# Two seams of a three-stage attention kernel: gate placement, early pools, split softmax, mixing rows stored in SBUF

## The chip, the cores and the metric

The kernel runs on one core of a Trainium2 chip. A core has a matrix engine (TensorE, PE in the profile; its weight loads are shown as PEld), a vector engine (VectorE, DVE), an activation engine (ScalarE, ACT), a general engine (GpSimd, POOL) and a queue engine that issues most of the DMA transfers (SyncE, SP). They run side by side and wait for one another through semaphores; each takes its instructions strictly in the order in which they were put in its queue. SBUF is the on-chip memory of 128 partitions, PSUM the banks into which PE writes. The metric is the device time of one launch in microseconds (us); the time before is the median of three runs.

## What is computed

Input `x` is 4 x 192 x 128 x 128 in float32 (images, channels, rows, columns). Two layers follow each other. Cut to what matters:

```python
# layer 0: attention between channels (8 heads of 24 channels), over all 16384 pixels
q, k, v, l = split(depthwise3x3(conv1x1(x, w_qkv)), 4)
q = q / max(norm(q over pixels), 1e-12);  k likewise
attn = softmax((q @ k.T) * temperature)              # 24 x 24 for each image and head
t = fc2(relu(fc1(mean of l over the pixels)))
L = t * sigmoid(t)                                   # the gate, one number for each image and channel
y = conv1x1(L + attn @ v + x, w_proj) + L
# layer 1: neighbourhood attention, 6 heads, 3x3 neighbours at dilation 1, 2, 3, reflected borders
h = y + depthwise3x3(y, pos_w) + pos_b
q, k, v = conv1x1(h, qkv_w)
out = conv1x1(neighbourhood attention of q, k, v, proj_w)
```

## The kernel before

There are three stages, and each has to end, or nearly, before the next can begin.

**Stage 1, `project` (L220) and `plan_projection` (L260).** The images are taken in two pairs, and a pair in 32 bands of four rows: 64 bands n = 0 to 63. `loads` brings a band of x (`xt`, L272 and L274, three transfers; four buffers); PE makes q, k, v of it (`pu`, L280 to L294); ACT copies q and k (`us`, five buffers) and SP stores them to `qk_dram`; v goes into a ring of rows (`vboth`, `ring2`), and its depthwise 3x3 is run there, for most channels by DVE as one operation for each tap (`tap`, L327: accumulator `pa` and, at the last tap, `v_False`; the band's centre tap is ACT's, L320) and for the rest by ACT and POOL (`v_True`). The results go to `v_dram`. The order of instructions inside the stage is planned by hand: class `Schedule` (L35) takes items with engines, costs and due times and lists them, and class `Stage` (L137) owns the stage's pools and emits the list. Outside of such a plan the framework's own scheduler orders the instructions, and it may put a transfer whose memory is free among the transfers of an earlier stage.

Ahead of the stage the main function and `project` load all weights that they need, with those of the gate and `wp1`, `wp2` among them (L199, L207): eighteen transfers issued before the first `xt`. The rings are set to zero whole by POOL (L251). During the stage the sums of x that the gate needs are collected (`xsum`, `xcol`, `xrow`). After the plan has been emitted comes the gate, `gate_bias` (L448), once for each pair of images: sums over the taps; `pl`, four matmuls for each image (L471, L472), multiplied by DVE (L473); mean; `pf`, `pf2`, the two small layers (L479, L484); sigmoid by ACT (L487); `pb` (L494), which brings the gate through the projection, and a copy to `bias` (L495). Each step waits for the one before. It uses PSUM of its own, two banks.

**Stage 2, `channel_attention` (L498).** For each of eight heads `convolved` (L527) is run for q and for k. It makes the depthwise 3x3 as banded matmuls: six steps c2, each with a tile of band matrices (`band`, L538) and a tile of rows (`u`, L541), both in pools of three buffers; for each two channels 24 matmuls into two PSUM tiles `pc` (L554, pool of four banks), which ACT copies (L563) and of which DVE takes the statistics (L565, for the norms). These ACT copies come in groups of four. `cut_rows` (L577) handles the two rows where the halves of the image meet. `products` (L618) multiplies q and k over all pixels (`gram`, L623, 128 matmuls), adds up the parts (`kept`, `part`, `extra`, `own`), and brings sums and squared norms through one PSUM tile `sm` (L645) into `logits`, `nk`, `nq` (L654 to L656).

When all eight heads are done, the softmax of all of them runs at once (L665 to L682: square root, maximum, reciprocal, three multiplications, maximum, subtraction, exponential, sum, reciprocal, multiplication). Then for each image the attention matrices go through the projection (`pm`, L689, two heads a PSUM tile), DVE copies them to `mixed` (L690, one buffer), and three transfers bring them to `mix_dram` and from there to `mix1` (rows 0 to 127) and `mix2` (64 rows behind `wp2`), L691 to L693. `mix1` and `mix2` hold the matrix by which one product takes the place of attention times v and projection.

**Stage 3, `second_pass` (L696).** Its own pools, its own plan. It loads the second layer's weights (L716 to L718), adds 1 to the centre tap (L719), sets its rings and `parts` to zero whole (L729, L1012), and then again walks over 64 bands: x and v of the band (`xv`, eight buffers, L733 to L744), the product with `mix1`, `mix2`, `wp1` (`ph`, L754), evicted by ACT with the gate's `bias` added (L758, `hboth`), positional taps, q, k, v, scores, softmax, sums over neighbours, output. The pools of this stage, and those of stage 2, take the memory that the stage before has used.

Of the kernel before, what the change touches and what calls it, by code (L numbers as in the profile page):

```python
# [14 lines left out]
HEADS0 = 8  # L15
# [19 lines left out]
class Schedule:  # L35
# [6 lines left out]
    def __init__(self):  # L42
        self.ops, self.pools = [], {}
# [93 lines left out]
class Stage:  # L137


    def __init__(self, ctx, tc, prefix, sbuf, psum):  # L140
        self.nc, self.bufs = tc.nc, {**sbuf, **psum}
        self.schedule, self.tiles, self.written, self.readers = Schedule(), {}, {}, {}
        self.pools = {}
        for n, k in self.bufs.items():
            space = dict(space=bass.MemoryType.PSUM) if n in psum else {}
            self.pools[n] = ctx.enter_context(tc.tile_pool(name=prefix + n, bufs=k, **space))
# [39 lines left out]
HALVES = [slice(0, G), slice(G, 128)]  # L186
AROUND = (0, 1, 2, 6, 7, 8, 3, 5)
# [3 lines left out]
def channel_attention_then_dilated_attention(ctx: ExitStack, tc: tile.TileContext, d, out: bass.AP):  # L191
# [10 lines left out]
    wp1 = load(const, "wp1")  # L202
    mix1, mix2, biases = [], [], []
    for b in range(B):
        mix1.append(const.tile([128, C], F32, tag=f"mix1{b}", name=f"mix1{b}"))
        mix2.append(const.tile([128, C], F32, tag=f"mix2{b}", name=f"mix2{b}"))
        nc.sync.dma_start(mix2[b][0:G], d["wp2"])  # L207
# [5 lines left out]
    mix_dram = dram.tile([B, C, C], F32, tag="mix_dram", name="mix_dram")  # L213

    project(tc, d, x, load, qk_dram, v_dram, v2_dram, biases)
    channel_attention(tc, d, load, qk_dram, mix_dram, mix1, mix2)
    second_pass(tc, d, x, load, wp1, mix1, mix2, biases, v_dram, v2_dram, out)


def project(tc, d, x, load, qk_dram, v_dram, v2_dram, biases):  # L220

    nc = tc.nc
    with ExitStack() as ctx:
        wts = ctx.enter_context(tc.tile_pool(name="p1w", bufs=1))
        st = ctx.enter_context(tc.tile_pool(name="p1s", bufs=2))

        wx, wx2, wv2, dwv = (load(wts, n) for n in ("wx", "wx2", "wv2", "dwv"))
        wl, wl2, dwl = load(wts, "wl"), load(wts, "wl2"), load(wts, "dwl")  # L230
        wprojI, wprojT = load(wts, "eye"), load(wts, "wprojT")
        fc1T, bfc1, fc2T, bfc2 = (load(wts, n) for n in ("fc1T", "bfc1", "fc2T", "bfc2"))
        nc.vector.tensor_add(wprojI, wprojI, wprojT)
        sums = []
        for p in range(B // 2):
            xsum = st.tile([128, 3, NB], F32, tag="xsum", name=f"xsum{p}")
            xcol = st.tile([128, 3, 2, H], F32, tag="xcol", name=f"xcol{p}")
            xrow = st.tile([128, 3, 3], F32, tag="xrow", name=f"xrow{p}")
            nc.gpsimd.memset(xrow, 0.0)
            sums.append((xsum, xcol, xrow))  # L240

        with ExitStack() as inner:
            stage = Stage(
                inner, tc, "p1", dict(xt=4, us=5, v=3, v2=3, side=3, ring=1), dict(pu=6, pa=1)
            )
            rings = stage.pools["ring"]
            vboth = rings.tile([128, RING + SPARE, 2, W + 2], F32, tag="vboth", name="vboth")
            ring = [vboth[:, :, 0], vboth[:, :, 1]]
            ring.append(rings.tile([128, RING + SPARE, W + 2], F32, tag="ring2", name="ring2"))
            for r in (vboth, ring[2]):  # L250
                nc.gpsimd.memset(r, 0.0)  # L251
            plan_projection(nc, stage, x, wx, wx2, wv2, dwv, vboth, ring, sums, qk_dram, v_dram, v2_dram)
            stage.run(tc)

        ps_g = ctx.enter_context(tc.tile_pool(name="p1pg", bufs=2, space=bass.MemoryType.PSUM))
        for p in range(B // 2):
            gate_bias(nc, st, ps_g, p, *sums[p], wl, wl2, dwl, fc1T, bfc1, fc2T, bfc2, wprojI, biases[p])
# [189 lines left out]

def gate_bias(nc, st, ps_g, p, xsum, xcol, xrow, wl, wl2, dwl, fc1T, bfc1, fc2T, bfc2, wprojI, bias):  # L448


    small = lambda shape, name: st.tile(shape, F32, tag=name, name=f"{name}{p}")
    tot = small([128, 3], "tot")
# [13 lines left out]
    for im in range(2):  # L466
        half = slice(im * G, (im + 1) * G)
        pl = ps_g.tile([HALF, 2, NT], F32, tag="pg", name=f"pl{p}_{im}")
# [8 lines left out]
    pf = ps_g.tile([RED, 2], F32, tag="pg", name=f"pf{p}")  # L477
# [4 lines left out]
    pf2 = ps_g.tile([HALF, 2, 2], F32, tag="pg", name=f"pf2{p}")  # L482
# [6 lines left out]
    pb = ps_g.tile([128, NG], F32, tag="pg", name=f"pb{p}")  # L489
# [8 lines left out]
def channel_attention(tc, d, load, qk_dram, mix_dram, mix1, mix2):  # L498
# [7 lines left out]
    with ExitStack() as ctx:  # L506
        wts = ctx.enter_context(tc.tile_pool(name="paw", bufs=1))
        band_p = ctx.enter_context(tc.tile_pool(name="pab", bufs=3))
        u_p = ctx.enter_context(tc.tile_pool(name="pau", bufs=3))
        cut_p = ctx.enter_context(tc.tile_pool(name="pac", bufs=1))  # L510
        q_p = ctx.enter_context(tc.tile_pool(name="paq", bufs=1))
        k_p = ctx.enter_context(tc.tile_pool(name="pak", bufs=1))
        st = ctx.enter_context(tc.tile_pool(name="pas", bufs=1))
# [5 lines left out]
        same, fold, ones, ident = load(wts, "same"), load(wts, "fold"), load(wts, "ones"), load(wts, "ident")  # L519
        wph, tempr = load(wts, "wph"), load(wts, "temp")  # L520
# [97 lines left out]
        def products(hd, q, sq, k, sk, cut):  # L618
# [25 lines left out]
            sm = ps_s.tile([CH0, 2 * B * CH0 + B], F32, tag="sm", name=f"sm{hd}")  # L644
# [12 lines left out]

        for hd in range(HEADS0):
            q, sq = convolved(hd, 0, q_p)
            k, sk = convolved(hd, 1, k_p)  # L660
            products(hd, q, sq, k, sk, cut_rows(hd, (sq, sk)))

        for n in (nq, nk):  # L665
            flat = n.rearrange("p b h -> p (b h)") if n is nq else n.rearrange("p b h c -> p (b h c)")
            nc.scalar.activation(flat, flat, AF.Sqrt)
            nc.vector.tensor_scalar_max(flat, flat, 1e-12)
            nc.vector.reciprocal(flat, flat)
        nc.vector.tensor_mul(nq, nq, tempr.unsqueeze(1).to_broadcast([CH0, B, HEADS0]))  # L670
        nh = B * HEADS0
        rows = logits.rearrange("p b h c -> p (b h) c")
        wide = lambda a: a.unsqueeze(2).to_broadcast([CH0, nh, CH0])
        nc.vector.tensor_mul(rows, rows, nk.rearrange("p b h c -> p (b h) c"))
        nc.vector.tensor_mul(rows, rows, wide(nq.rearrange("p b h -> p (b h)")))
        top, tot = fin.tile([CH0, nh], F32, tag="top", name="top"), fin.tile([CH0, nh], F32, tag="tot", name="tot")
        nc.vector.tensor_reduce(top, rows, AX.X, ALU.max)
        nc.vector.tensor_sub(rows, rows, wide(top))
        nc.scalar.activation(rows, rows, AF.Exp)
        nc.vector.reduce_sum(tot, rows, axis=AX.X)  # L680
        nc.vector.reciprocal(tot, tot)
        nc.vector.tensor_mul(rows, rows, wide(tot))  # L682
        for b in range(B):
            mixed = fin.tile([CH0, HEADS0, C], F32, tag="mixed", name=f"mixed{b}")
            for hd in range(0, HEADS0, 2):
                pm = ps_c.tile([128, B, W], F32, tag="pc", name=f"pm{b}_{hd}")
                two = pm.rearrange("p b w -> p (b w)")[:CH0, : 2 * C].rearrange("p (h o) -> p h o", h=2)
                for e in range(2):
                    nc.tensor.matmul(two[:, e, :], logits[:, b, hd + e, :], wph[:, hd + e, :], start=True, stop=True)  # L689
                nc.vector.tensor_copy(mixed[:, hd : hd + 2, :], two)  # L690
            nc.sync.dma_start(mix_dram[b].rearrange("(h c) o -> c h o", c=CH0), mixed)  # L691
            nc.sync.dma_start(mix1[b], mix_dram[b, 0:128, :])
            nc.sync.dma_start(mix2[b][G:128], mix_dram[b, 128:C, :])  # L693


def second_pass(tc, d, x, load, wp1, mix1, mix2, biases, v_dram, v2_dram, out):  # L696
# [4 lines left out]
    with ExitStack() as ctx:  # L701
# [6 lines left out]
                xv=8, y=3, y2=3, prod=3, middle=2, side=1, moved=1, term=4, acc=4, o=3, s_sb=1, e=2, mx=2, sm=2, e_sb=2,  # L708
            ),
            dict(pc=2, ex=2, q=1, pa=1, sc=1),  # L710
        )
        add, hold, tile_of, tiles = stage.schedule.add, stage.hold, stage.tile, stage.tiles
        fill, read, repeat, written = stage.fill, stage.read, stage.repeat, stage.written
        wts, rings = pool("p2w", 1), pool("p2r", 1)

        wq1, wq2, wkv, wkv2 = (load(wts, n) for n in ("wq1", "wq2", "wkv", "wkv2"))  # L716
        wo, wo2, posw, posb = (load(wts, n) for n in ("wo", "wo2", "posw", "posb"))
        pick, order, spread = (load(wts, n) for n in ("pick", "order", "spread"))  # L718
# [9 lines left out]
        for r in (hboth, hring[2]):  # L728
            nc.gpsimd.memset(r, 0.0)  # L729
# [281 lines left out]
        for t in parts:  # L1011
            nc.gpsimd.memset(t, 0.0)  # L1012
# [295 lines left out]
def build(arrays):  # L1308
    import concourse.bacc as bacc

    nc = bacc.Bacc("TRN2", target_bir_lowering=False, num_devices=1)
# [17 lines left out]
```

## Time and profile before

| | |
|---|---|
| median of three runs | 4686.12 us (4683.99 to 4691.63) |
| the profiled execution | 4694.5 us, its span 4692.7 us |
| mean granted TensorE clock | 0.979 |
| PE busy | 4494.9 us, 96% of the span |
| DVE, POOL, ACT busy | 3919.5 (84%), 3229.8 (69%), 2784.3 us (59%) |
| stage 1 | to about 857 us |
| stage 2 | 901 to about 1717 us, eight heads |
| stage 3 | from about 1765 us to the end |

The span is the time from the first to the last event of the profiled execution; the execution's own time is some 2 us longer. The page divides the span into 40 slices of 117.3 us and shows the busy share of each in tenths, where 9 is 90% or more. These are the rows of TensorE, the clock that it was granted, and what the transfers moved:

```profile
PE   8999999799999988999999999999999999999986
PEclk9999999899999988999999999999999999999997
DMA  7777777688877845444344444434444444443311
GB/s 225 244 242 234 237 238 237 165 186 183 181 170 163 179 100 136 91 105 101 91 95 104 101 98 100 105 93 97 105 96 97 105 101 91 107 102 89 91 43 30
```

The eighth slice (821 to 938 us) holds the first seam, the fifteenth (1642 to 1760 us) most of the second: there PE drops to 7 and 8 tenths. In slices of this width the rest is full. A TensorE that counts as busy isn't necessarily at its peak, since the records of matmuls overlap.

### The profile page before, as it was taken

What the parts mean: (1) busy time and instruction counts of PE and PEld (TensorE: products, weight loads), DVE (VectorE), ACT (ScalarE), POOL (GpSimd) and SP (SyncE); (2) the same over time, 40 slices, a digit from 0 to 9 for tenths busy, and PEclk for the clock granted to TensorE, in tenths of its full rate; (3) what the DMA queues carried; (4) which work ended last, traced back from release to release, by engine and by line L of the source; (5) the groups of instructions that cost most, each with busy time, mean ns of one, the idle gap of its engine ahead of it and who ended that gap; (6) DMA issues with size and microseconds to landing.
All of it is one profiled execution on the core that took longest, in us unless ns stands there. A gap on an engine that the chain in (4) does not pass through costs nothing.

```text
span 4692.7 us, 63172 instructions
## 1 busy us (share of the span) xinstructions
PE 4494.9 (96%) x20592; PEld 1640.0 (35%) x20592; DVE 3919.5 (84%) x5480; ACT 2784.3 (59%) x4759; POOL 3229.8 (69%) x2765
## 2 busy tenths in 40 slices
PE   8999999799999988999999999999999999999986
PEld 3333333344455442233333333333333333333321
DVE  6998899655444545899999999999999999999996
ACT  6888888666656646455455555555555555555531
POOL 6787778400000002788889999898899999999997
PEclk9999999899999988999999999999999999999997
DMA  7777777688877845444344444434444444443311
GB/s 225 244 242 234 237 238 237 165 186 183 181 170 163 179 100 136 91 105 101 91 95 104 101 98 100 105 93 97 105 96 97 105 101 91 107 102 89 91 43 30
DMA packets 496615, 628.31 MB, mean 134 GB/s; under 512 B 136144, under 2 KB 331036, under 8 KB 496288
## 3 DMA queue, kind: packets, MB, share of 16 engines
q1 hardware_dynamic: 476832, 524.40, 42.1%
q0 software_dynamic: 19456, 99.89, 11.1%
q8 instruction: 165, 2.70, 0.3%
q14 instruction: 162, 1.33, 0.1%
HBM read 297.18 MB, written 201.92 MB: 106 GB/s over the span
## 4 chain that ended last, share of the span: by engine, by line
PE 69%; DVE 14%; DMA 5%; issue 5%; POOL 3%; ACT 2%; SPq 1%; POOLq 0%; DVEq 0%; ACTq 0%
PE ph L754 9%; PE pc L554 8%; PE pu L280 7%; PE ex L1097 7%; PE sc L973 6%; DVE prod L962 6%; DVE term L1103 5%; PE pu L285 4%; PE gram L623 4%; PE po L1119 3%; PE po L1115 3%; PE pkv L896 3%; POOL acc L1106 3%; PE pu L413 2%; PE q L951 2%
## 5 line engine op out<-in xcount | busy, mean ns | idle before, releaser
L1106 POOL TENSOR_TENSOR acc<-acc,term 128x512 f32<-128x512 f32 x1536 | 1977.2, 1289 | 215.0 <-DVE term L1103 139.1
L1103 DVE TENSOR_TENSOR term<-ex,vring 128x512 f32<-128x512 f32 (+2 forms) x1596 | 1007.4, 661 | 67.0 <-PE ex L1097 39.7
L962 DVE TENSOR_TENSOR prod<-q,kring 128x1536 f32<-128x1536 f32 (+1 forms) x600 | 1008.3, 1686 | 34.0 <-ACT kring L914 13.9
L350 POOL TENSOR_TENSOR v_True<-v_True,side 128x512 f32<-128x512 f32 (+1 forms) x512 | 647.9, 1267 | 189.3 <-ACT side L339 162.2
L563 ACT COPY conv<-pc 128x512 f32<-128x512 f32 x384 | 511.2, 1501 | 267.1 <-PE pc L554 244.2
L327 DVE SCALAR_TENSOR_TENSOR pa<-vboth,dwv,pa 128x1024 f32<-128x1024 f32 (+1 forms) x448 | 574.3, 1282 | 86.2 <-ACT pa L320 56.0
L1097 PE MATMUL ex<-e_sb,spread 108*128 108x512 bf16 x1728 | 596.0, 387 | 46.2 <-DVE term L1103 20.7
L554 PE MATMUL pc<-u,band 64*64 64x508 f32 (+1 forms) x4608 | 581.5, 596 | 30.4 <-DMA band<-in_bands 12.1
L729 POOL MEMSET hboth<- 128x3900 f32 x1 | 3.3, 3347 | 874.9 <-DMA mix_dram<-mixed 874.9
L565 DVE BATCH_NORM_STATS2 stats<-pc 128x6 f32<-128x128 f32 x1536 | 341.9, 285 | 256.3 <-ACT conv L563 256.3
L809 DVE SCALAR_TENSOR_TENSOR pa<-hboth,posw,pa 128x1024 f32<-128x1024 f32 (+1 forms) x384 | 489.5, 1275 | 65.8 <-ACT pa L797 52.7
L973 PE MATMUL sc<-prod,pick 128*32 128x512 f32 x3456 | 483.8, 607 | 4.0 <-DVE e L1030 2.8
L1097 PEld LDWEIGHTS <-spread 108*128 108x128 bf16 x1728 | 149.1, 98 | 723.3 <-issue 689.8
L896 PE MATMUL pkv<-y,wkv 128*128 128x512 f32 x768 | 390.5, 620 | 8.3 <-ACT kring L909 2.7
L833 ACT ACTIVATE side<-hring,posw 128x512 f32<-128x512 f32 x512 | 335.2, 710 | 101.5 <-DMA side<-side 79.0
L754 PE MATMUL ph<-xv,mix 128*128 128x512 f32 (+1 forms) x1024 | 386.1, 609 | 5.3 <-DMA xv<-v_dram 4.5
L280 PE MATMUL pu<-xt,wx 128*128 128x512 f32 x768 | 365.8, 612 | 14.3 <-DMA xt<-in_x 14.3
L909 ACT COPY kring<-pkv 64x512 f32<-64x512 f32 x384 | 223.1, 581 | 224.6 <-PE pkv L899 211.7
L339 ACT ACTIVATE side<-ring,dwv 128x512 f32<-128x512 f32 (+1 forms) x512 | 349.9, 735 | 6.0 <-POOL v_True L350 5.4
L554 PEld LDWEIGHTS pc<-u,band 64*64 64x64 f32 x4608 | 216.5, 133 | 382.8 <-issue 259.8
L1122 ACT COPY o<-po 128x512 f32<-128x512 f32 x192 | 106.2, 588 | 306.6 <-PE po L1115 206.5
L298 ACT COPY us<-pu 128x512 f32<-128x512 f32 x384 | 203.5, 601 | 90.8 <-PE pu L285 90.8
(158 smaller groups left out, 5913.2 us busy)
## 6 DMA issues: line engine op xcount, KB each, us to landing
qk_dram<-us SPq DMA_DIRECT2D x192, 512.0 KB
u<-qk_dram SPq DMA_DIRECT2D x384, 256.0 KB
side<-side POOLq DMA_DIRECT2D x124, 768.0 KB, 5.8
band<-in_bands SPq DMA_DIRECT2D x192, 192.0 KB
xt<-in_x SPq DMA_DIRECT2D x64, 512.0 KB
v_dram<-v_False SPq DMA_DIRECT2D x64, 512.0 KB
xv<-in_x SPq DMA_DIRECT2D x128, 256.0 KB
xv<-v_dram SPq DMA_DIRECT2D x128, 256.0 KB
```

The costliest lines, as they stand in the source:

```text
L280: mm(pu, wx[:, mt * 128 : (mt + 1) * 128], tiles["xt", n][:, im, :], start=True, stop=False)
L327: nc.vector.scalar_tensor_tensor(by_row(to[:, o : o + length]), by_row(vboth[:, at : at + length, :, t % 3 : t % 3 + W]), dwv[:, 0, t : t ...
L350: nc.gpsimd.tensor_add(v[:, rows, :], v[:, rows, :], z[:, rows, :])
L554: nc.tensor.matmul(pcs[e][r * G : (r + 1) * G, :, to], band[at, e, c, dx, :], u[at, e, c, :].rearrange("p (b w) -> p b w", w=W)[:, :, of], ...
L563: nc.scalar.copy(full[:, :, :, ch], pcs[e])
L754: mm(to, w[:, cols], tiles["xv", n, j, im], start=j == 0, stop=j == 2)
L896: mm(rows3(tile_of("pc", key)), w, tiles["y", n, im], start=True, stop=False)
L962: nc.vector.tensor_mul(to[:, :, px].rearrange("p t (r w) -> p t r w", w=W), q.unsqueeze(1).to_broadcast([128, 3, *q.shape[1:]]), three,)
L973: mm(sc[quad * 32 : (quad + 1) * 32, :], pick[:, QR - 4 * row : QR - 4 * row + 32], tiles["prod", n, k // NT, k % NT // 3][:, k % 3, :], s ...
L1097: mm(rows3(tile_of("ex", ("ex", n, g, t))), spread[:, t, :], e_sb, start=True, stop=True)
L1103: nc.vector.tensor_mul(rows3(to[:, px]), rows3(ex[:, px]), win)
L1106: nc.gpsimd.tensor_add(tiles["acc", n, g], tiles["acc", n, g], tiles.pop(("term", n, g, t)))
```

## The change

In the words of the code, it does the following.

- `Stage` can be given ready-made pools. The pools of `xv` and of the third stage's weights (`wts2`) are taken before everything else, those of `band`, `u`, the gate's weights and the gate's small tiles before stage 1 and kept until the end of stage 2.
- Ahead of stage 1 only `wx`, `wx2`, `wv2`, `dwv` are loaded. `us` has six buffers in the place of five.
- Rings are set to zero in their two border columns only, `parts` in its last columns only.
- The gate is called from `channel_attention` after the second head (`meanwhile(1, ...)`), and its PSUM tiles are taken from the tag `sm` of that stage, which has one bank. After the third head `wp2` and the third stage's weights are loaded in program order (`meanwhile(2, ...)`); the framework may put these transfers earlier.
- `finish(first, end)` is the softmax and the mixing for a range of heads. It is called for heads 0 to 6 after head 6, and for head 7 at the end. `mixed` now holds one head for all images ([24, 4, 192], one buffer), and four transfers a head (eight for head 5, whose rows are split between `mix1` and `mix2`) bring it straight to `mix1` and `mix2`; `mix_dram` is gone.
- The memory for DMA descriptors is given as 8192.

```diff
-            for r in (vboth, ring[2]):
-                nc.gpsimd.memset(r, 0.0)
...
+    wts2, xv_p = (ctx.enter_context(tc.tile_pool(name=n, bufs=k)) for n, k in (("p2w", 1), ("p2xv", XV)))
+    with ExitStack() as early:
+        band_p, u_p = (early.enter_context(tc.tile_pool(name=n, bufs=3)) for n in ("pab", "pau"))
+        gate_w = early.enter_context(tc.tile_pool(name="p1g", bufs=1))
+        gate_p = early.enter_context(tc.tile_pool(name="p1s", bufs=2))
...
+        project(tc, x, load, sums, qk_dram, v_dram, v2_dram)
+
+        def meanwhile(hd, ps):
+
+            if hd == 1:
+                gates(nc, gate_w, gate_p, ps, load, sums, biases)
+            if hd == 2:
+                for b in range(B):
+                    nc.sync.dma_start(mix2[b][0:G], d["wp2"])
+                w2.update({n: load(wts2, n) for n in SECOND})
+
+        w2 = {}
+        channel_attention(tc, d, load, qk_dram, mix1, mix2, band_p, u_p, meanwhile)
+    second_pass(tc, x, w2, xv_p, mix1, mix2, biases, v_dram, v2_dram, out)
...
-                inner, tc, "p1", dict(xt=4, us=5, v=3, v2=3, side=3, ring=1), dict(pu=6, pa=1)
...
+        stage = Stage(ctx, tc, "p1", dict(xt=4, us=6, v=3, v2=3, side=3, ring=1), dict(pu=6, pa=1))
...
+        for r in ring:
+            nc.gpsimd.memset(r[:, :, 0 : W + 2 : W + 1], 0.0)
...
+def gates(nc, wts, st, ps_g, load, sums, biases):
+    wl, wl2, dwl, wprojI, wprojT = (load(wts, n) for n in ("wl", "wl2", "dwl", "eye", "wprojT"))
+    fc1T, bfc1, fc2T, bfc2 = (load(wts, n) for n in ("fc1T", "bfc1", "fc2T", "bfc2"))
+    nc.vector.tensor_add(wprojI, wprojI, wprojT)
+    for p, bias in enumerate(biases):
+        gate_bias(nc, st, ps_g, p, *sums[p], wl, wl2, dwl, fc1T, bfc1, fc2T, bfc2, wprojI, bias)
...
+    sums = lambda name: ps_g.tile([128, SM], F32, tag="sm", name=name)
...
-        pl = ps_g.tile([HALF, 2, NT], F32, tag="pg", name=f"pl{p}_{im}")
+        pl = sums(f"pl{p}_{im}")[:HALF, : 2 * NT].rearrange("p (m t) -> p m t", m=2)
...
+        def finish(first, end):
+
+
+            n = end - first
+            own = slice(first, end)
...
+            for hd in range(first, end):
+                mixed = fin.tile([CH0, B, C], F32, tag="mixed", name=f"mixed{hd}")
+                for b in range(0, B, 2):
+                    pm = ps_c.tile([128, B, W], F32, tag="pc", name=f"pm{hd}_{b}")
+                    two = pm.rearrange("p b w -> p (b w)")[:CH0, : 2 * C].rearrange("p (h o) -> p h o", h=2)
+                    for e in range(2):
+                        nc.tensor.matmul(two[:, e, :], logits[:, b + e, hd, :], wph[:, hd, :], start=True, stop=True)
+                    nc.vector.tensor_copy(mixed[:, b : b + 2, :], two)
+                for b in range(B):
+                    low = min(max(128 - hd * CH0, 0), CH0)
+                    if low:
+                        nc.sync.dma_start(mix1[b][hd * CH0 : hd * CH0 + low], mixed[:low, b, :])
+                    if low < CH0:
+                        at = G + hd * CH0 + low - 128
+                        nc.sync.dma_start(mix2[b][at : at + CH0 - low], mixed[low:, b, :])
+
         for hd in range(HEADS0):
             q, sq = convolved(hd, 0, q_p)
+            if hd == 0:
+                same, fold, ones, ident, wph, tempr = (load(wts, n) for n in "same fold ones ident wph temp".split())
             k, sk = convolved(hd, 1, k_p)
             products(hd, q, sq, k, sk, cut_rows(hd, (sq, sk)))
...
+            meanwhile(hd, ps_s)
+            if hd == HEADS0 - 2:
+                finish(0, HEADS0 - 1)
+        finish(HEADS0 - 1, HEADS0)
...
-        for n in (nq, nk):
-            flat = n.rearrange("p b h -> p (b h)") if n is nq else n.rearrange("p b h c -> p (b h c)")
-            nc.scalar.activation(flat, flat, AF.Sqrt)
...
-        for b in range(B):
-            mixed = fin.tile([CH0, HEADS0, C], F32, tag="mixed", name=f"mixed{b}")
...
-            nc.sync.dma_start(mix_dram[b].rearrange("(h c) o -> c h o", c=CH0), mixed)
-            nc.sync.dma_start(mix1[b], mix_dram[b, 0:128, :])
-            nc.sync.dma_start(mix2[b][G:128], mix_dram[b, 128:C, :])
...
+            dict(xv=xv_p),
...
+        wp1, wq1, wq2, wkv, wkv2, wo, wo2, posw, posb, pick, order, spread = (w2[n] for n in SECOND)
...
-            nc.gpsimd.memset(t, 0.0)
+            nc.gpsimd.memset(t[:, :, :, 3 * GT :], 0.0)
...
+    nc = bacc.Bacc("TRN2", target_bir_lowering=False, num_devices=1, dynamic_dma_scratch_size=8192)
```

## The prediction

> **What bounds the kernel now.** I read the table of busy time by stretches first, for where TensorE (PE) is kept busy and where not (columns: stretch, its us; busy us and count of each engine; granted clock; DMA share; GB/s).
>
> ```profile
> core 0: us, PE busy (x) PEld busy (x) DVE busy (x) ACT busy (x) POOL busy (x), PEclk, DMA share, GB/s
> 500.00:857.00 357.00, 357.00 (x1028) 127.34 (x1026) 321.89 (x254) 314.24 (x541) 284.80 (x289) 1.00 0.70 232
> 857.00:901.00 44.00, 13.93 (x82) 12.56 (x80) 23.33 (x33) 18.36 (x30) 22.73 (x20) 0.55 0.38 112
> 901.00:987.00 86.00, 82.70 (x609) 33.91 (x610) 46.11 (x202) 64.51 (x51) 0.00 (x0) 0.97 1.08 221
> 1291.00:1391.00 100.00, 98.19 (x872) 51.83 (x871) 49.78 (x216) 65.77 (x51) 0.00 (x0) 1.00 0.83 179
> 1717.00:1765.00 48.00, 26.14 (x91) 11.86 (x89) 22.50 (x38) 3.09 (x4) 2.42 (x1) 0.55 0.32 83
> ```
>
> Stage 1 (the projection) is PE-bound with DMA at 0.70; the attention's first head (901–987) is DMA-bound; the steady head (1291–1391) is not. Between the stages lie two seams at half clock, 857–901 and 1717–1765, with PE busy 14 of 44 and 26 of 48 us. The third stage is untouched by the diff but for its start. So I read the seams and one steady head in the timeline (columns: start, us, engine, line, operation, [idle before <- what released it]).
>
> ```profile
> 874.24 2.98 PE L494 MATMUL pb<-gate,eye 96*128 96x1 f32 x16 [10.78 <-DVE gate L488]
> ...
> 892.99 1.28 DVE L327 SCALAR_TENSOR_TENSOR v_False<-vboth,dwv,pa 128x1024 f32<-128x1024 f32 x1
> 901.52 8.78 PE L554 MATMUL pc<-u,band 64*64 64x512 f32 x52 [12.08 <-DMA band<-in_bands]
> 906.76 3.99 ACT L563 COPY conv<-pc 128x512 f32<-128x512 f32 x3 [21.95 <-DMA band<-in_bands]
> ```
>
> Seam 1: the gate's small operations sit between the last depthwise taps on DVE, and the convolution waits for loads that start only when the stage's memory is free.
>
> ```profile
> 1188.78 20.73 PE L623 MATMUL gram<-conv,conv 128*96 128x96 f32 x242
> 1209.54 0.55 DVE L626 TENSOR_TENSOR kept<-gram,same 96x384 f32<-96x384 f32 x1 [18.46 <-PE gram L623]
> 1214.40 5.27 ACT L563 COPY conv<-pc 128x512 f32<-128x512 f32 x4 [24.84 <-PE pc L554]
> ```
>
> A steady head: from the gram's end (1209.4) to the next head's first copy 5.0 us; then 4 copies x 1.32 + 0.46 = 5.74 us a group, and 74.4 to the next gram when no load is late.
>
> ```profile
> 1717.18 0.55 DVE L626 TENSOR_TENSOR kept<-gram,same 96x384 f32<-96x384 f32 x1 [18.46 <-PE gram L623]
> 1720.35 0.14 DVE L656 COPY nq<-sm 24x4 f32<-24x4 f32 x1
> ...
> 1723.51 4.93 DVE L669 RECIPROCAL nk<-nk 24x768 f32<-24x768 f32 x1
> ...
> 1735.85 20.64 PE L689 MATMUL pm<-wph,logits 24*24 24x192 f32 x64 [15.88 <-DVE logits L682]
> 1737.33 0.55 DVE L690 COPY mixed<-pm 24x384 f32<-24x384 f32 x1 [1.62 <-PE pm L689]
> ...
> 1744.15 1.47 DVE L690 COPY mixed<-pm 24x384 f32<-24x384 f32 x3 [2.44 <-DMA mix_dram<-mixed]
> ...
> 1767.05 0.69 ACT L758 ACTIVATE hboth<-ph,bias 128x512 f32<-128x512 f32 x1 [33.67 <-PE ph L754]
> ```
>
> Seam 2: softmax of all heads 18.7 us after the gram (ended 1717.15), then mixing rows, where the `mixed` buffer costs 2.44 us for its store; the third stage's first eviction comes 49.9 us after the gram, band 1's (1779.89) 62.7.
>
> **The change, part by part** (against the profiled span 4692.7, whose run took 4694.5, 8.4 above the median 4686.12; I apply the sum to the median).
>
> *Start.* Before, 18 weight DMAs at 0.43 us stand ahead of the first xt (issued 9.83; PE at 14.28, 4.45 later). In the built order four are left: issue at ~3.1, PE at ~7.5. Stage 1 is PE-bound, so **-6.8** (5 to 7.5).
>
> *Seam 1.* Without gate operations the tail of the taps runs: band 62's centre 860.40 + 1.14, eight taps to 872.1, band 63's centre to 873.3, taps 9.6, end 883.2 (now 894.27). Bands and half the rows of u are loaded before that, in memory of their own. What sets the end is then the first ACT copy, whose target lies where the taps' weights lie: 883.2 - 6.8 = 876.4. From there the steady 74.4 plus ~3 for a cold PE gives gram 0 at 953.8, where it began at 986.92: **-33 with the start** (-25 if half the first head's DMA-bound stretch stays, -36 without the cold PE).
>
> *Early transfers.* Some 48 DMAs (bands, tap tables, gate and third-stage weights, eight xv tiles; 5.3 MB) go into SP's queue among stage 1's xt, us and v transfers. I take **0**: SP waits 522 of 857 us, DMA share is 0.70, xt has four buffers at 13 us a band. Uncovered, they cost 5.3 MB / 238 GB/s = 22.
>
> *Gate in head 2.* In the built order gate work is in line, not beside: after head 1's sums PE takes pl, pl, pf, pf2, pb for each image pair, each waiting for DVE, through one PSUM bank, with some 26 convolution matmuls (0.13 us busy each) between them in all; ACT's copies queue behind those and DVE's statistics. One pair took 877.14 to 889.64 = 12.5 at half clock; shortening pl and pb to their warm rows but adding the table load, ~11 each. From the gram: 3.3 (sums) + 22 + ~3.5 for statistics between = 29 until the fifth ACT copy, which normally comes at 10.7; cold restart 2: **+20** (12 if one pair hides behind the first group, 26 if pairs take 12.5 and hops lengthen). The head's transfers don't make it up: their share is 0.96 in a conv phase.
>
> *Seven heads after head 6.* All 28 mixing matmuls stand ahead of head 7's first convolution on PE. After gram 6: 3.3 to the sums, 1.7 for square roots and table load, 7/8 of 12.3 (1723.43 to 1735.71) = 10.8, so pm at 15.8, first copy 17.3, second 19.2. Then each head waits for the four small DMAs of the head before: two copies 1.2 + issues 0.45 + 2.4 (row of 1744.15) = 4.05; head 5, whose rows split, has eight DMAs, 5.75. Banks free for the convolution at ~38.9, third ACT copy near 48 where it normally is at 7.9: **+41** (33 if the wait is 1.2, 47 if 3.4).
>
> *Seam 2.* For one head the operations on 24x96 fall to their floors (reciprocal 4.93/8 = 0.6): pm ~10.8 after the gram, rows in place ~15.2, first eviction ~17.3 for 49.9. Band 1's then follows by 9.7 (12.8 before, less most of the 3.51 wait for xv, since three of its xv tiles or more are in memory) at 27 for 62.7: **-36** (-30 to -40). Behind that the third stage's order is unchanged.
>
> *Sixth us buffer, smaller memsets, DMA scratch*: **0**; no ACT copy in stage 1 waits for us, and the memsets (3.35, 1.72 us) lie on idle POOL; if a border column were late it would cost one memset, 3.3.
>
> [...]
>
> Sum: -33 + 0 + 20 + 41 - 36 = **-8**; 4686.1 - 8 = **4678**. Half-widths 5.5, 5, 7, 7, 5, combined as independent, are 13: the likeliest case's own range is 4665 to 4691.
>
> **Rivals.**
> (a) *The insertions hide more than half.* If the framework's PE queue lets the convolution run beside, gate +8 and seven heads +25: sum -36, 4650; between, 4662. For it: ACT, POOL and most of DVE are idle there, and a straight DMA may be shorter than the 2.44 of a store. Against: the PE order puts the chain ahead.
> (b) *Stage 1 is starved* (slower). The 48 transfers push xt back in SP's queue and the shared DMA engines; price 22, and 4678 + 22 = 4700. It decides once PE loses 18 us waiting for xt in the first ten bands. For it: SP issues in order, and a transfer with an unmet wait blocks those behind. Against: xt's slack of three bands, 39 us.
> (c) *Early memory isn't early in effect*: the first convolution still waits for loads, as 901.52 did, so head 0 stays DMA-bound and its copy comes 12 us later: sum +4 to +7, 4692.
> (d) *The insertions are dearer*: small DMAs at 3.4 each and gate 26: sum +4, 4690.
>
> **How the numbers follow.** Chances: forecast 0.52, (a) 0.23, (b) 0.10, (c) 0.07, (d) 0.08. A measurement of this kernel tells about 0.2% (9.4 us) from no change: 4676.7 and 4695.5 are the bounds. Forecast case: 0.45 faster, 0.52 same, 0.03 slower; (a) faster; (b) mostly slower; (c), (d) mostly same with a fifth slower. Faster 0.46, same 0.40, slower 0.14. The range takes the likeliest's own and reaches into (a) and (c): 4660 to 4695.
>
> **What would show it.** In the profile after: xt issued near 3 and PE from 7.5; stage 1's period still 13 us with no DMA wait on PE; the last tap ~876 and gram 0 near 954; between gram 1 and head 2's fifth ACT copy ~29 us; after gram 6 a gap of ~47 to the third copy, `mixed` copies released by DMA about 2.4 each; after gram 7 the first eviction at ~17. The prediction is wrong if PE waits for xt in stage 1, if a gap is under half of its term, or if the first head keeps 80 us.

## The result, and the profile after

| | median | runs | profiled execution |
|---|---|---|---|
| before | 4687.17 us | 8, 4683.99 to 4691.63 | 4694.5, span 4692.7 |
| after | 4700.81 us | 8, 4696.86 to 4707.08 | 4700.0, span 4698.2 |

The changed kernel is slower: the ratio is 1.0030, with a 95% interval of 1.0020 to 1.0041. The forecast was 4678 with a range of 4660 to 4695.

The windows view of after, in the columns that were explained above:

```profile
500.00:857.00 357.00, 355.64 (x1046) 126.49 (x1046) 320.24 (x253) 314.42 (x541) 284.89 (x288) 1.00 0.74 240
857.00:901.00 44.00, 21.62 (x176) 9.11 (x172) 32.11 (x74) 32.00 (x34) 19.46 (x16) 0.77 0.60 150
1080.00:1112.00 32.00, 31.33 (x130) 15.96 (x132) 5.88 (x32) 7.44 (x7) 0.00 (x0) 0.53 0.15 39
1627.00:1666.00 39.00, 27.11 (x100) 12.88 (x104) 8.84 (x22) 2.71 (x2) 0.00 (x0) 0.55 0.05 14
```

Stage 1 still keeps PE full (355.6 of 357) while it carries the early transfers; PE's only wait for `xt` in it is the first one, 7.8 us. The first seam holds more work than before (PE busy 21.6 of 44 us, where it was 13.9). And there are two new holes in stage 2. The third row is the trap of this profile: PE is shown busy 31.3 of 32 us, yet the granted clock is 0.53 and ACT has done 7 instructions. The busy share alone doesn't show this hole; the clock and the engine that uses PE's results do.

Where the time went is read best from one mark for each head, the start of `kept` (the DVE operation that ends a gram), taken from the timeline of each run:

```
         head 0   then the period of heads 1 to 7                     first eviction of stage 3
before   1007.5   99.3 102.7 102.5  99.8  99.9 102.6 102.8            49.9 behind the last mark
after     975.2  101.3 131.8 100.9 101.3 100.8 100.2 149.0            15.3
```

Head 0 is 32.3 us earlier, head 2 loses 29.1, head 7 loses 46.2, the other five differ by 0.4 in sum, and the seam behind the last gram is 34.6 us shorter to the first eviction, 37.1 to that of band 1 (1786.03, 25.6 behind the gram, for 62.7). Band 1's eviction is then 6.1 us later than before, and the span ends 5.5 us later: stage 3 is unchanged.

The first seam in the timeline of after:

```profile
876.74 1.28 DVE L332 SCALAR_TENSOR_TENSOR v_False<-vboth,dwv,pa 128x1024 f32<-128x1024 f32 x1
878.18 5.26 ACT L573 COPY conv<-pc 128x512 f32<-128x512 f32 x4 [3.54 <-DVE v_False L332]
```

The first convolution's copy is released by the last tap, no longer by the load of bands: 878.2 where 876.4 was worked out and 906.8 stood before.

### The profile page after: what moved, and what is told of

Same layout as the page of the kernel before. It is cut to its first block, busy times and chain, and to the rows that moved or that the text cites. A ratio compares the mean times of both kernels' runs of the same rounds, so it can differ in the third digit from the quotient of the medians.

```text
span 4698.2 us, 63217 instructions
## 1 busy us (share of the span) xinstructions
PE 4502.7 (96%) x20592; PEld 1645.5 (35%) x20592; DVE 3920.5 (83%) x5492; ACT 2788.9 (59%) x4764; POOL 3219.9 (69%) x2767
## 4 chain that ended last, share of the span: by engine, by line
PE 68%; DVE 15%; issue 5%; DMA 4%; POOL 4%; ACT 3%; SPq 1%; POOLq 0%; DVEq 0%; ACTq 0%
PE ph L776 9%; PE pc L564 8%; PE pu L285 7%; PE ex L1119 7%; PE sc L995 6%; DVE prod L984 6%; DVE term L1125 5%; PE pu L290 4%; PE gram L633 4%; PE po L1141 3%; PE po L1137 3%; PE pkv L918 3%; POOL acc L1128 3%; PE pu L418 2%; PE q L973 2%
## 5 line engine op out<-in xcount | busy, mean ns | idle before, releaser
L1119 PE MATMUL ex<-e_sb,spread 108*128 108x512 bf16 x1728 | 596.6, 387 | 46.2 <-DVE acc L1125 21.3
L564 PE MATMUL pc<-u,band 64*64 64x508 f32 (+1 forms) x4608 | 591.7, 604 | 47.1 <-DVE stats L575 28.1
```

Of the source, the lines that this page charges most:

```text
L564: nc.tensor.matmul(pcs[e][r * G : (r + 1) * G, :, to], band[at, e, c, dx, :], u[at, e, c, :].rearrange("p (b w) -> p b w", w=W)[:, :, of], ...
L1119: mm(rows3(tile_of("ex", ("ex", n, g, t))), spread[:, t, :], e_sb, start=True, stop=True)
```

## Experiments

Two theories stood against each other after the result. By the *queue theory* the gate and the seven heads cost their whole chain because they stand in line on PE and DVE with the convolution behind them. By the *work theory* PE is full anyway, so the work costs the same wherever it stands. Each kernel below changes the changed kernel; times are medians, the ratio is to runs of the kernel before that were taken beside it.

**1 to 4: the two insertions, spread out or taken back.**

```diff
 # e1: gate_bias as a generator, one step after every two channels of head 2
+                    next(beside, None)        # in convolved, behind the statistics of a group
 # e2: softmax and rows of heads 0 to 6 the same way in head 7, products in the bank of sm
+                    pm = ps_s.tile([128, SM], F32, tag="sm", name=f"pm{hd}_{b}")
 # e3: both.   e4: the gate behind stage 1, as before the change
+        with tc.tile_pool(name="p1pg", bufs=2, space=bass.MemoryType.PSUM) as ps_g:
+            gates(nc, gate_w, gate_p, ps_g, load, sums, biases)
```

> The changed kernel with the same gate operations issued one step after every two channels of head 2's convolutions (PE, DVE and ACT in a fixed order there), so that each step's input is two groups old. Queue theory (the gate cost 29 us in the changed kernel because its chain stands in line with the convolution behind it): head 2 gets back 20 to 26 us, its period goes from 131.8 to 106-112, time near 4678. Work theory (PE is 98 of 100 us busy in a head, so the gate's matmuls and the broken rhythm cost the same wherever they stand): under 10 us come back, period over 122, time over 4690. Elsewhere theory (the loss is in stage 1 or 3): period shorter, time unchanged.

> The changed kernel with the softmax and the mixing rows of seven heads issued one step after every two channels of head 7's convolutions, the products in the PSUM bank of the sums in place of the convolution's four. Queue theory: head 7's period goes from 149 to 108-116 (own PE time of 28 products at 0.16 x 2 us, two table loads of 1.28), time near 4665. Work theory: at most a third of the 46 us comes back, period over 132, time over 4685.

> Both spreads together. Queue theory: the sum of the two gains, 50 to 60 us, time 4640 to 4650, faster than the kernel before by 0.8 to 1.0%. Work theory: at most 25 us, time over 4675.

> The changed kernel with only the gate put back behind stage 1, with two PSUM banks of its own as before; the early memory stays. Queue theory: head 2 back to 101 (29 us less), the last taps later by the 11 us that the gate cost there before (first ACT copy near 889 in place of 878), net -18, time near 4683. Work theory: the gate hides in neither place, head 2 gives 29 back and the seam takes 25 or more, time 4697.

Measured:

```
                   time us   ratio (interval)           head 0   head 2   head 7
after              4700.81   1.0030 (1.0020-1.0041)      975.2    131.8    149.0
e1 gate spread     4687.13   1.0006 (0.9995-1.0016)      976.2    115.6    149.6
e2 rows spread     4733.93   1.0104 (1.0081-1.0126)      976.1    127.8    186.1
e3 both            4718.17   1.0071 (1.0051-1.0092)      976.1    115.6    184.4
e4 gate at seam    4686.43   1.0000 (0.9990-1.0009)      988.3    103.2    150.0
```

The gate. Spreading takes 16.2 us off head 2 and 13.7 off the time, between the two theories. (In e2, e5, e6 and e7, which keep the gate as built, head 2 took 127.8 to 130.3, so up to 4 of its 29 us are scatter.) The timeline of after shows why the line was so dear (PE, then one row of ACT):

```profile
1079.30 1.07 PE L564 MATMUL pc<-u,band 64*64 64x508 f32 x4
...
1084.57 1.96 PE L564 MATMUL pc<-u,band 64*64 64x508 f32 x4
1086.46 0.25 PE L493 MATMUL pf<-pool,fc1T 96*12 96x2 f32 x4
...
1111.56 10.23 PE L564 MATMUL pc<-u,band 64*64 64x508 f32 x66
1121.99 5.58 PE L564 MATMUL pc<-u,band 64*64 64x512 f32 x48 [0.20 <-DVE stats L575]
...
1115.24 2.71 ACT L573 COPY conv<-pc 128x512 f32<-128x512 f32 x2 [7.21 <-PE pc L564]
```

Between two gate steps PE runs a set of four convolution matmuls alone. At 1079.30, with the clock still at 1.00, such a set took 1.07 us; from 1082 on, at 0.50, it took 1.96. In the stream from 1121.99, at full clock, 48 take 5.58, 0.47 for four. So the lone set cost 2.3 times its price in the stream, and half clock nearly doubled that. PE hardly waits, 0.5 us in all; it is slow. The account closes: from 1079.30 to 1111.56 are 32.3 us, of which ten sets (eight of four and two of eight) take 18.4 and the gate's own matmuls 13.4. The 48 matmuls of the sets would have taken 5.6 in the stream, and the 66 that follow, at a granted clock of 0.79, take 10.2 in place of 7.7. That makes 12.8 + 13.4 + 0.5 + 2.5 = 29.2, and head 2 lost 29.1. What makes a lone set dear no run isolates. The gate's 96- and 128-row matmuls stand on both sides of it here, but a set was dear without them too: at 1175.41 and 1478.28 two convolution matmuls, with only others of their kind around them and waits of 0.2 to 0.4 us for `u` on both sides, took 1.04 us at full clock. Why the clock fell while the records show PE busy stays open. The fifth ACT copy came 38.8 us behind the gram (1115.24 against 1076.4), not 29.

In e1 the steps stand whole groups apart and the clock is 0.92 from 1080 to 1112 and 0.98 from there to 1160, in place of 0.53. What is left shows as gaps on ACT at the steps, and as the gate's own time:

```profile
1094.24 0.34 PE L497 MATMUL gate_pl<-reach,wl 128*96 128x9 f32 x2
...
1152.68 3.50 PE L544 MATMUL gate_bank<-gate,eye 96*128 96x1 f32 x32
...
1093.56 2.71 ACT L663 COPY conv<-pc 128x512 f32<-128x512 f32 x2 [1.65 <-PE pc L654]
1100.88 5.27 ACT L663 COPY conv<-pc 128x512 f32<-128x512 f32 x4 [4.61 <-PE pc L654]
```

Its PE time is about 9 us (two `gate_pl` blocks of 2.1, 0.3, 0.8, 3.5) in a head whose PE has none to spare (98.2 of 100 us busy in a steady head of before): this half of the work theory holds. At the seam (e4) PE idles anyway (22.4 of 44 us in after), and there the gate makes the first copy come at 888.6, as its queue theory said (889), and head 0 end 13.1 us later (9 to 14 over e4, e8 and e11, which have it there), but nothing after that: as good as the spread, and 14.4 us better than after.

The rows. Both theories missed e2, which lost 33 us. The reason is in its own order:

```profile
1694.96 1.44 PE L754 MATMUL pm<-wph,logits 24*24 24x192 f32 x4 [4.27 <-DVE mixed L756]
1696.33 4.70 PE L565 MATMUL pc<-u,band 64*64 64x512 f32 x24
1705.30 1.44 PE L754 MATMUL pm<-wph,logits 24*24 24x192 f32 x4 [4.27 <-DVE mixed L756]
...
1701.08 2.71 ACT L574 COPY conv<-pc 128x512 f32<-128x512 f32 x2 [7.63 <-PE pc L565]
```

Each product needs the one bank that the `mixed` copy before it empties, and that copy stands on DVE behind the statistics of the group that PE has only just finished. So PE can't run ahead: a group takes 10.3 us in place of 2.87. A second bank for the products was not tried. The softmax part, which has no product, cost little: 14 pairs of copies in 46.4 us, 3.3 a pair. Spread steps had to be spaced by what stood ahead of them in the queue of the engine that feeds them (4.27 us of waiting at each product), not by their number. e3 is the sum of e1 and e2: -13.7 + 33.1 = +19.4, measured +17.4.

**5 to 7: what head 7's 46 us are made of.**

```diff
 # e5
-                mixed = fin.tile([CH0, B, C], F32, tag="mixed", name=f"mixed{hd}")
+                mixed = fin.tile([CH0, B, C], F32, tag="mixed", name=f"mixed{hd}", bufs=2)
 # e6
-            if hd == HEADS0 - 2:
-                finish(0, HEADS0 - 1)
-        finish(HEADS0 - 1, HEADS0)
+        finish(0, HEADS0)
 # e7: mix1 and mix2 of the four images in one tile each, [128, B, C]
-                for b in range(B):
...
+                    nc.sync.dma_start(mix[0][hd * CH0 : hd * CH0 + low], mixed[:low])
```

> The changed kernel with two buffers for mixed in place of one. Store theory (of the 46 us that head 7 lost, five heads' waits of 4.0 us for the four stores of the head before are 20, and what stays is the softmax chain of 15.5 and the products at half clock): a head's rows take 2.6 us (two copies at the products' 1.28) in place of 5.0, head 7's period goes from 149 to 136-139, time near 4689. Rival (the stores' issue on SP, four at 0.65 = 2.6 a head, then sets the pace anyway, with waits left on DVE): 3 to 4 us a head, period 140-145, time 4693 to 4697.

> The changed kernel with the seven heads not finished early: one softmax and all rows after head 7, the straight stores and one buffer kept. Queue theory: head 7 back to 101 (48 less); behind the gram 18.7 for the softmax, 1.5 to the first copy, eight heads at 5.0 and one double one, 4 for the last stores, then 2.7: first eviction near 66 in place of 15.3, +50. Net +2, time 4703: finishing early as built gains nothing. Rival (finishing early is worth what it takes off the seam, and the straight stores are quick): at least 20 slower than the changed kernel, 4721.

> The changed kernel with the matrices of the four images side by side in one tile, so that a head's rows are stored by one transfer in place of four (two in place of eight for head 5). Issue theory (of the 4.0 us wait 1.3 is the issue of the last two transfers, and landing takes 2 to 2.7): wait 2.6 to 2.9, head 7's period 149 to 140-143, time near 4693; seam 2 shorter by 1 to 2 us too. Rival (landing time is all of it): no change, 4700.

Measured: e5 4689.05 us (ratio 1.0001, 0.9991 to 1.0012), head 7 135.3; e6 4698.48 (1.0031, 1.0020 to 1.0042), head 7 100.0, first eviction 61.3 behind the gram; e7 4689.34 (1.0011, 1.0001 to 1.0020), head 7 136.0. The rows of `mixed` on DVE, in after, e5 and e7 in turn:

```profile
1648.80 1.01 DVE L699 COPY mixed<-pm 24x384 f32<-24x384 f32 x2 [3.95 <-DMA mix<-mixed]
1653.86 1.01 DVE L699 COPY mixed<-pm 24x384 f32<-24x384 f32 x2 [4.05 <-DMA mix<-mixed]
...
1661.90 1.01 DVE L699 COPY mixed<-pm 24x384 f32<-24x384 f32 x2 [0.36 <-DVE stats L575]
```

```profile
1645.02 1.01 DVE L699 COPY mixed<-pm 24x384 f32<-24x384 f32 x2 [2.12 <-PE pm L698]
1648.10 1.01 DVE L699 COPY mixed<-pm 24x384 f32<-24x384 f32 x2 [2.07 <-DMA mix<-mixed]
```

```profile
1639.08 1.01 DVE L700 COPY mixed<-pm 24x384 f32<-24x384 f32 x2 [2.42 <-DMA mix<-mixed]
1642.47 1.01 DVE L700 COPY mixed<-pm 24x384 f32<-24x384 f32 x2 [2.38 <-DMA mix<-mixed]
```

A head took 5.0 us with four stores and one buffer, 3.1 to 3.3 with two buffers once both are in use, 3.4 with one store. The wait of 2.4 that the prediction took from the old store is the price of one transfer; four in a row cost 4.0. e5's heads stay above the copies' pace of 2.6, as its rival said, but period and time are those of the store theory. In e7 the wait fell to 2.4, a little below what the issue theory said; the period gained more than it allowed, 13 us. Five waits shorter by 1.6 are 8 of it; 3.5 more came since head 5's eight stores became two: head 6's copies (the row of 1661.90 in after) stood 8.0 us behind head 5's in after and 4.5 in e7. e6 shows what finishing early was worth as built: without it the time is 2.3 us lower, which can't be told from nothing, as its queue theory expected. The 46.0 us that the last seam saved by it (61.3 against 15.3) were paid as 49.0 in head 7.

**8, 10, 11: a version that beats both.** What each engine does at the place was read from the profile: behind stage 1 PE idles 22.4 of 44 us; around a gram DVE idles 18.5 us and ACT 24.8 (the wait before 1213.07); behind the last gram PE waits 4.2 us for the last head's softmax (`pm` at 1767.38).

```diff
 # e8: gate as in e4, one store as in e7, two buffers, and
+        softmax(0, last)                                   # DVE and ACT, ahead of the last gram
+        products(last, q, sq, k, sk, cut, some)            # some: three products behind extra
+        softmax(last, HEADS0, some)
+        for _ in tiles:                                    # the rest of the 28, copied by ACT
+            pass
 # e10: besides, the last k convolution to the end in emission order on DVE and ACT,
 #      and the gate's steps between the last taps in a fixed order;  e11: the first of these alone
+        early.enter_context(tc.manual_schedule(engines={mybir.EngineType.DVE, mybir.EngineType.Activation}))
```

> A version put together from the theory: gate behind stage 1 (as in the fourth run), seven heads' softmax on DVE and ACT ahead of or during the last gram, where both wait for PE, their 28 products behind the gram while the last head's softmax runs, copied by ACT, one store a head, two buffers. Queue theory: head 7's period 101 to 107, first eviction 22 to 28 after the gram in place of 15.3, with the gate's 15 back: 4700.8 - 15 - 45 + 10 = 4650, faster than the kernel before by 0.7 to 0.9%. Work theory: the chain costs its time wherever it stands, time over 4675.

> The version of the eighth run with two orders written out by hand: the gate's steps put between the last taps of stage 1, far enough apart that DVE never waits for PE, and the seven heads' softmax held back to the last gram, where DVE and ACT idle. Queue theory: first ACT copy 5 us earlier (884 in place of 888.9, the gate's own 4 us of DVE stay), head 7's period 101 in place of 107.9; 4651.6 - 5 - 7 = 4640. Work theory: both costs only move, no change, 4650.

> The version of the eighth run with only the second of the two orders by hand: the seven heads' softmax held back to the last gram, the gate behind stage 1 as the framework puts it. Queue theory: head 7's period 101 in place of 107.9 and everything else as in the eighth run, 4651.6 - 6.5 = 4645. Rival (the seam behind the gram takes back what head 7 gains, since the products' inputs are ready later): 4651.

```
                        time us   ratio (interval)           head 0   head 7   first eviction
e8  rows in gram        4651.59   0.9931 (0.9916-0.9945)      984.4    107.9    25.1
e10 gate in tail        4656.81   0.9945 (0.9929-0.9962)      993.3    101.4    23.4
e11 softmax in gram     4650.28   0.9919 (0.9902-0.9936)      989.0    101.7    23.3
```

e8 gives what the queue theory said (4650), 0.69% less than the kernel before: the seven heads cost 7 us in head 7 and 10 behind the last gram, where in line they cost 46. Its last seam:

```profile
1698.66 0.55 DVE L637 TENSOR_TENSOR kept<-gram,same 96x384 f32<-96x384 f32 x1 [18.41 <-PE gram L634]
1699.05 2.13 PE L704 MATMUL pm<-wph,logits 24*24 24x192 f32 x12
...
1701.72 15.64 PE L704 MATMUL pm<-wph,logits 24*24 24x192 f32 x52
...
1717.40 0.55 DVE L705 COPY mixed<-pm 24x384 f32<-24x384 f32 x1 [0.68 <-PE pm L704]
...
1723.72 0.69 ACT L799 ACTIVATE hboth<-ph,bias 128x512 f32<-128x512 f32 x1 [8.41 <-PE ph L795]
```

The 28 products of the seven heads now take the place in which the last head's softmax ran alone; the eviction is 9.8 us later than in after, and head 7 is 41 shorter. The scheduler had put the seven heads' softmax into the start of head 7 and not into the gram. e10 and e11 hold it back, and head 7 falls to 101.4 and 101.7 as expected; the seam took nothing back. Yet e11's time, 4650.28, can't be told from e8's: six microseconds are inside the scatter of the rest. Head 0 ends 4.5 us later in e11's profile, with the same code up to there, and the other heads' periods are 99.5 to 103.7 in e11's profile and 100.6 to 102.0 in e8's. e10's gate went the wrong way (timeline of e10):

```profile
857.74 1.23 DVE L492 TENSOR_TENSOR cut<-cut,xcol 128x3 f32<-128x3 f32 x1
...
887.02 5.89 PE L548 MATMUL gate_rest<-gate,eye 96*128 96x1 f32 x32 [6.59 <-DVE gate L541]
893.32 6.78 PE L658 MATMUL pc<-u,band 64*64 64x512 f32 x48 [0.41 <-DVE bias L552]
```

The gate's preparing operations, which after and e8 have hidden inside stage 1 (those of the second pair near 816), now stood in the fixed order between the last taps, 12.7 us from 855.9 to 868.5, and the last tap began at 889.3, 1.9 later than in e8 and not earlier. (Seven of these 23 small operations took 1.1 to 1.2 us, as that of 857.74 did; such a subtraction took 0.16 in e8, at 809.18. Why, no run shows.) And the gate's last matmuls, now those of both pairs in one block at 887.02, stood on PE ahead of the convolution, which began at 893.3 in place of 884.1. The first copy came at 897.6, not 884.

**9: the kernel before once more.**

> The kernel before once more, for a second profile of it. Profile theory (the profiled execution of before, 4694.5, was one of the slow ones of its spread, and the sum of 5.5 us between the two profiles is 8 short of the 13.6 between the medians for that reason alone): this profile lies within 4683 to 4690, and the difference sits in the heads, whose periods of 102.5 to 102.8 become 99 to 100 in more of the eight. Rival (a profile of this kernel always costs 8): again 4693 to 4696.

This execution took 4689.86 (span 4688.1), with periods of 100.3 to 102.2 between heads 1 and 7: inside the range of the profile theory, but only at its upper end. The four heads that had 102.5 to 102.8 are 6.1 us shorter in sum, but none comes under 100, the other three are 3.2 longer and head 0 ends 0.9 later. So the last gram ends 2.1 us earlier, and 2.5 are gained behind it.

## Why the prediction was wrong, step by step

- **Start and seam 1, -33:** right, -32.3. xt was issued at 2.61, PE began at 7.79, the last tap ended at 878.0 and gram 0's main part began at 954.4 (forecast near 3, 7.5, 876, 953.8). For the 3 us of a cold PE the forecast names no row, and no run shows the term by itself; in after the first 52 convolution matmuls (880.69) took 7.91, 1.9 more than at the 5.54 of 48 in the stream, with a granted clock of 0.52 to 884 and 1.00 from there. Rival (c) fell: the first copy waits for the last tap, not for a load.
- **Early transfers, 0:** right. PE stayed full in stage 1 at a DMA share of 0.74 and never waited for `xt` after the first; rival (b), which had named 4700 by starvation, had the number and not the cause. The order in SP's queue that it names does show in after: a `us` store whose copies had ended at 505.77 was issued at 510.05, behind an `xt` that waited for PE until 508.39.
- **Gate in head 2, +20:** mis-sized, +29.1 (25 to 29 over the five runs that keep this gate). The step that failed is "some 26 convolution matmuls (0.13 us busy each)", 3.4 us: that is their price in a stream. The rows show 48 of them in ten sets, 18.4 us, up to 1.98 a set. That the chain stands in line was right; that each step waits for DVE was not, since the sets fill those waits: PE waited 0.5 us, and the two pairs, set down at 22, took 13.4 of matmuls of their own. For the 2 of a cold restart it names no row either; the 66 matmuls behind the gate took 2.5 more than in the stream.
- **Seven heads, +41:** mis-sized, +46.2. The step that failed is the wait of 2.4 taken from one store; four stores in a row waited 4.0, and the cycle was 5.0, not 4.05. Five cycles put the convolution's start at 43.0 behind the gram, not 38.9. Head 5's eight stores were mis-sized too (7.0 from copy to copy in e6, not 5.75): PE waited another 3.1 for head 6's copies, and the third ACT copy came at 55.4, not 48. About 1 us of that came back by the end of the head. e5 and e7 shorten the waits and gain 11.8 and 11.5.
- **Seam 2, -36:** right, -37.1 (15.3 and 25.6 behind the gram, forecast 17 and 27).
- **Sixth buffer, memsets, scratch, 0:** nothing in the trace speaks against it; not tried alone.
- **The sum** was -8 and is +6.1 in the trace, 14 off: 9 from the gate and 5 from the rows. That is rival (d)'s mechanism, insertions dearer, which got a chance of 0.08; of its bounds of 26 and 47 the gate passed the first.
- **From the sum to the median:** the other 8 us. The two profiles differ by 5.5, the medians by 13.6, since the profiled execution of before lay 7.3 above its median and that of after 0.8 below. A second profile of before lay 3 to 5 above. Against that second profile the same marks give +10.1 for the whole span, with 31.0 for the gate and 48.6 for the seven heads, so 4.6 of the 8 came with the profile against which the terms were read: its heads 2 and 7 were long ones. The step that failed here is "I apply the sum to the median". What makes before longer when it is profiled stays open; its two profiles differ by 4.6 us, about as much as the sum that was to be told.

The table loads on ACT, 1.28 us each, moved next to nothing. In both softmaxes of after (1615.61 and 1764.09) they lay beside DVE work; in the gate the load of 1090.08 held the sigmoid until 1091.37, and PE waited 0.5 us behind it.

## What to carry to other kernels

Work that was moved "beside" a loop ran beside it here only where the queues that it entered had idle time at that spot: look for the engine's idle stretch in the timeline (here behind stage 1 for PE, during a gram for DVE and ACT) and move the chain there, since in line it cost its whole length here (46 us for the seven heads, 17 in the idle stretches of e8). Price a matmul that is cut out of its stream by a row in which it stands alone (here 1.07 us for four in place of 0.47), and a group of stores by a row with as many stores (here a wait of 4.0 us for four, 2.4 for one). When gains and losses of 30 to 50 us nearly cancel, the difference carries the errors of all of them, here 9 and 5 us on a sum of 8, and the range has to be as wide.

## What the runs showed of the hardware that was not expected

Four 64 x 64 convolution matmuls between others took 1.07 us at full clock and 1.96 at a granted clock of 0.50, and 0.47 in a stream at full clock. TensorE was granted 0.53 of its clock over 32 us in which the records show it busy for 31.3. Four stores of 24 x 192 from one tile held its buffer for 4.0 us behind the last copy, one store of the same bytes for 2.4.
